# A graph network layer pair: the first phase's order written by hand, with counting spread between product matmuls

## The chip, the cores and the metric

The kernel runs on one NeuronCore of one Trainium2 chip. The metric is the device time of one execution in microseconds (us). Several executions are timed and their median is given; one further execution is recorded by the hardware profiler, and all lines of a profile come from that one.

## The reference, cut to what matters

There are 1250 nodes with 1024 features and 41,250 edges, sorted by destination. The first layer is a relational graph convolution, the second an attention layer over the same edges.

```python
h = relu(layernorm(x))                       # 1250 x 1024
nx = ln_weight * h * rsqrt(mean(h*h) + 1e-6)
out = nx @ W_root + bias                     # 1024 -> 286
for r in range(2):                           # mean over the edges of each relation
    msg = nx[src] @ W_rel[r] * (edge_type == r)[:, None]
    out += segment_sum(msg, dst) / maximum(count_r, 1)
x = x + h + elu(out) @ wo                    # 286 -> 1024
h = relu(layernorm(x))
g = h @ W                                    # 1024 -> 1024
e = exp(-leaky_relu(al[src] + ar[dst]))      # al, ar: g times two vectors
x = x + elu(segment_sum(e * g[dst], src) / (segment_sum(e, src) + 1e-5))
```

## The kernel before, in words

The 1250 nodes lie in ten tiles of up to 128 rows (T = 10, KD = 8 blocks of 128 features). A preparation sorts the edges into 110 groups of three chunks of 125 edges (NG = 110, J = 3) and makes, for each edge, a key and a low number. Then comes `fast_arm`, whose first phase (lines 469 to 572) does two independent things.

*Counting.* For each group, `count(q)` builds the number of edges between nodes as products of one-hot matrices. For each of its three chunks VectorE writes a one-hot `key` (line 496, 125 x 320, in five rotating buffers), and every two groups a one-hot `lo` (line 479). TensorE multiplies the two into `acc` (line 497), and one more matmul of 20 columns, the carry (line 500), adds what belongs to the last node of the group before. ScalarE loads the group's first node into a register (line 501) and evicts the sum of the group to that place of `cnt` (line 503). The carry's one-hots, `hot_ck`, are made in two pieces (line 486), for groups 0 to 9 and for the rest.

*Products.* For each tile, `norms` takes the statistics of x on VectorE (line 441), a square root on ScalarE, a reciprocal and `nmr` on VectorE (446, 448), then h = relu(layernorm(x)) on ScalarE (450) and the sum of its squares (510, 512). `turn` transposes h in eight matmuls (460) and copies the result to hT, one half on each of ScalarE and VectorE (463, 465). `products` multiplies hT with the joined weights wcat in sixteen steps (r = 0 and 1, k = 0 to 7, line 521; each is two matmul instructions of 429 columns in the profile). From the result, VectorE makes y0, the root part with bias (526), and the relation part is split into three bf16 parts: the first on ScalarE (531), the rest on VectorE (533), the second on ScalarE (535), the third on VectorE (536). GpSimd writes a column of ones (537). `residual` adds h to x on VectorE (554), as the sum of both is needed later. The norm's weight is multiplied into wcat ahead of all products, eight times on ScalarE (561).

The order of the instructions on each engine is that of the scheduler, which starts from the order of the calls (`some(1)` to `some(4)` groups between the stages of a tile) and moves instructions by its own estimate of when they are ready. In the order that it makes, many products stand one after the other (nine in a row at the end of most tiles), and counting stands in bunches between others. PSUM has two banks for each of two products ("mm"), three banks shared by transpositions and sums of counting ("tp"), and one that every fourth group uses ("own").

After the phase, the weights of the second layer are loaded over wcat on SP's queue (580), wo on ScalarE's (591, 598), and `means` (line 629, 600 matmuls) multiplies the counts with the bf16 parts of y. VectorE prepares wo (600 to 605) and the columns of scores (617), and the way back to 1024 columns (669) is added to x (671). The second layer's product, weights and sums follow; the change doesn't touch them.

Of the kernel before, what the change touches and what calls it, by code (L numbers as in the profile page):

```python
# [410 lines left out]
def fast_arm(tc, ctx, w_root, conv_bias, wo, w_gat, a_gat, out,  # L411
# [25 lines left out]
    def norm_relu(work, xt, n):  # L437

        st = sm.tile([128, 2, 6], F32, name="st")
        for i in range(2):  # L440
            nc.vector.bn_stats(st[:n, i, :], xt[:n, i * 512:(i + 1) * 512])  # L441
# [8 lines left out]
        nc.scalar.activation(h[:n], xt[:n], AF.Relu, bias=nmr[:n], scale=rstd[:n])  # L450
        return h

    def transposed(work, h, n, turn):

        hT = work.tile([128, KD, 128], F32, name="hT", bufs=2)
        for g in range(KD // 4):
            pt = bank("tp")
            for i in range(4):
                k = 4 * g + i
                nc.tensor.transpose(pt[:, i, :n], h[:n, k * 128:(k + 1) * 128], ident[:n, :n])  # L460
            o = hT[:, 4 * g:4 * g + 4, :n]
            if (g + turn) % 2 == 0:
                nc.scalar.activation(o, pt[:, :, :n], AF.Copy)
            else:
                nc.vector.tensor_copy(o, pt[:, :, :n])  # L465
        return hT


    y0s, ybs = {}, {}
    with ExitStack() as c1:  # L470
        hot = c1.enter_context(tc.tile_pool(name="hot", bufs=5))
        work = c1.enter_context(tc.tile_pool(name="work1", bufs=2))
        los = {}

        def count(q):

            if q % 2 == 0:
                los[q // 2] = hot.tile([PE_, 128, 2 * J], BF16, name="lo", bufs=2)
                nc.vector.tensor_tensor(  # L479
                    los[q // 2], iota_lo,  # L480
                    lows[:, q:q + 2, :].rearrange("p q j -> p (q j)")[:, None, :].to_broadcast([PE_, 128, 2 * J]),
                    ALU.is_equal,
                )
            if q in (0, 10):
                q1 = 10 if q == 0 else NG
                nc.vector.tensor_tensor(hot_ck[:, q:q1], iota_ck[:, None, :].to_broadcast([PE_, q1 - q, 2 * T]),
                                        ck[:, q:q1, None].to_broadcast([PE_, q1 - q, 2 * T]), ALU.is_equal)
            acc = (own_bank if q % 4 == 3 else bank)("acc").rearrange("p a b -> p (a b)")
            a3 = acc[:, :2 * T * W].rearrange("p (c w) -> p c w", w=W)
            if q:  # L490

                last = los[(q - 1) // 2][:, :, ((q - 1) % 2) * J + J - 1]
                carry = (a3[:, :, 0:1], last, hot_ck[:, q - 1, :, None])
            for j in range(J):
                key = hot.tile([PE_, 2 * T * W], BF16, name="key")
                nc.vector.tensor_scalar(key, iota_key, keys[:, q, j:j + 1], None, op0=ALU.is_equal)  # L496
                nc.tensor.matmul(acc[:, :2 * T * W], los[q // 2][:, :, (q % 2) * J + j], key, start=(j == 0),  # L497
                                 stop=(j == J - 1))
                if q and j == 0:
                    nc.tensor.matmul(*carry, start=False, stop=False)  # L500
            b = nc.values_load(bases[0:1, q:q + 1], engines=[mybir.EngineType.Activation],  # L501
                               min_val=0, max_val=N - 1)
            nc.scalar.activation(cnt_w[:, :, bass.ds(b, W)], a3, AF.Copy)  # L503

        def norms(t):
            n = ROWS[t]
            h = norm_relu(work, xs[t], n)
            sq = work.tile([128, D], F32, name="sq", tag="rest", bufs=1)
            ssq = small("ssq")
            nc.scalar.activation(sq[:n], h[:n], AF.Square, accum_out=ssq[:n])  # L510
            rms = small("rms")
            nc.scalar.activation(rms[:n], ssq[:n], AF.Sqrt, bias=eps6[:n], scale=1.0 / D)
            nc.vector.reciprocal(rms[:n], rms[:n])
            return h, rms

        def products(t, hT, rms):
            n = ROWS[t]
            py = ps.tile([128, 2, 512], F32, name="mm")
            for r in range(2):
                for k in range(KD):  # L520
                    nc.tensor.matmul(py[:n, r, :F + HF], hT[:, k, :n], wcat[k][:, r, :],  # L521
                                     start=(k == 0), stop=(k == KD - 1))
# [3 lines left out]
            nc.vector.scalar_tensor_tensor(  # L526
                y0[:n].rearrange("p (a b) -> p a b", a=2), py[:n, :, F:F + HF], rms[:n],
                bias[:n].rearrange("p (a b) -> p a b", a=2), op0=ALU.mult, op1=ALU.add,
            )

            nc.scalar.activation(yb[:n, 0, :, :F], py[:n, :, :F], AF.Copy, scale=rms[:n])
            rest = work.tile([128, D], F32, name="rest", tag="rest", bufs=1)[:, :2 * F].rearrange("p (r f) -> p r f", r=2)
            nc.vector.scalar_tensor_tensor(rest[:n], py[:n, :, :F], rms[:n], yb[:n, 0, :, :F],
                                           op0=ALU.mult, op1=ALU.subtract)
            nc.scalar.activation(yb[:n, 1, :, :F], rest[:n], AF.Copy)
            nc.vector.tensor_tensor(yb[:n, 2, :, :F], rest[:n], yb[:n, 1, :, :F], ALU.subtract)
            nc.gpsimd.memset(yb[:n, 0, :, F:F + 1], 1.0)

        groups = iter(range(NG))

        def some(n):
            for _ in range(n):
                q = next(groups, None)
                if q is not None:
                    count(q)

        hs_, hTs, rmss = {}, {}, {}

        def turn(t):
            hTs[t] = transposed(work, hs_[t], ROWS[t], t + 1)  # L550

        def residual(t):
            n = ROWS[t]
            nc.vector.tensor_add(xs[t][:n], xs[t][:n], hs_.pop(t)[:n])

        hs_[0], rmss[0] = norms(0)
        some(1)
        turn(0)
        hs_[1], rmss[1] = norms(1)
        for k in range(KD):  # L560
            nc.scalar.activation(wcat[k], wcat[k], AF.Copy, scale=lnw[:, k:k + 1])
            some(1)
        for t in range(T):
            residual(t)
            if t + 2 < T:
                hs_[t + 2], rmss[t + 2] = norms(t + 2)
            some(4)
            if t + 1 < T:
                turn(t + 1)
            some(3)  # L570
            products(t, hTs.pop(t), rmss.pop(t))
            some(4)

# [7 lines left out]
    work = ctx.enter_context(tc.tile_pool(name="work2", bufs=1))  # L581
# [21 lines left out]
    for i in (1, 3):  # L603
        p = slice(32 * i, 32 * i + 32)
# [311 lines left out]
    os_, oTs, hTs = {}, {}, {}  # L916

    def norm(t):
        hs_[t] = norm_relu(work, xs[t], ROWS[t])
# [4 lines left out]
    hs_ = {}  # L924
# [258 lines left out]
```

## Time and profile before

| what | value |
|---|---|
| median of 3 runs | 654.65 us (654.1 to 656.29) |
| the profiled execution | 655.82 us |
| its span | 654.0 us, so 1.8 us lie around it |
| granted TensorE clock, mean over the span | 0.987 |
| TensorE busy | 613.8 us, 94% |
| VectorE busy | 391.2 us, 60% |
| ScalarE busy | 191.8 us, 29% |
| GpSimd busy | 31.1 us, 5% |
| first key matmul of the first phase | at 15.27 us |
| first product matmul | at 27.41 us |
| first matmul of the means | at 208.59 us |

A row of the timeline gives start, duration, engine (PE is TensorE, PEld its weight loads, DVE is VectorE, ACT is ScalarE), the line of the kernel, the operation, output and inputs, shapes, and in brackets how long the engine had been idle and what ended that. Rows merge neighbouring instructions of one kind (x2, x8). Matmuls are pipelined and their ends are modelled, so what one costs is read from the distance between starts, not from its duration.

### The profile page before, as it was taken

How to read it: one execution, taken by the hardware profiler on the slowest of the kernel's cores; microseconds unless marked ns; L12 is line 12 of the kernel's file. 1: busy time of each engine (PE TensorE's matmuls, PEld its weight loads, DVE VectorE, ACT ScalarE, POOL GpSimd, SP SyncE). 2: the span in 40 equal slices, each digit the busy share in tenths (PEclk: the TensorE clock that was granted, in tenths of full speed). 3: DMA queues.
4: the chain of work that ended last, by engine and by line, in shares of the span. 5: the costliest groups of instructions: out<-in, count | busy, mean ns of one | idle time of the engine just before them, and what ended most of it. 6: DMA issues, size and time to landing. Idle time of an engine off the chain costs nothing.

```text
span 654.0 us, 7831 instructions
## 1 busy us (share of the span) xinstructions
PE 613.8 (94%) x2816; PEld 418.1 (64%) x2816; DVE 391.2 (60%) x947; ACT 191.8 (29%) x332; POOL 31.1 (5%) x42
## 2 busy tenths in 40 slices
PE   2589999999999989999799999999999999999995
PEld 1356665566665756676656788888866666666653
DVE  5599987777663399655873412214146666665632
ACT  3565555444432112420021122313112222222120
POOL 3000000000000000000000000000001111111110
PEclk9799999999999999999989999999999999999998
DMA  7900000000004610000730000000000000000011
GB/s 230 321 19 1 2 2 1 2 0 2 2 0 164 221 33 1 1 2 1 133 69 1 1 0 1 1 1 1 0 1 33 33 32 33 32 32 34 18 48 30
DMA packets 25209, 25.06 MB, mean 38 GB/s; under 512 B 14035, under 2 KB 18894, under 8 KB 25160
## 3 DMA queue, kind: packets, MB, share of 16 engines
q1 hardware_dynamic: 24059, 21.39, 10.7%
q10 hardware_dynamic: 1037, 2.90, 1.6%
q8 instruction: 24, 0.39, 0.3%
q14 instruction: 25, 0.20, 0.1%
q0 software_dynamic: 64, 0.17, 0.1%
HBM read 16.06 MB, written 5.12 MB: 32 GB/s over the span
## 4 chain that ended last, share of the span: by engine, by line
PE 80%; DVE 9%; DMA 6%; ACTq 2%; issue 1%; SPq 1%; ACT 1%; DVEq 0%
PE mm L898 16%; PE mm L521 14%; PE mm L774 11%; PE p L898 8%; PE mm L629 7%; PE acc L497 6%; PE mm L669 5%; PE z L774 4%; PE mm L703 3%; PE p L910 3%; DMA w<-in_L_gnn_W_rel_dram 2%; DVE scr L617 2%; ACTq L501 2%; DVE key L496 1%; PE p L703 1%; DMA rest_w<-in_L_gnn_wo_weight_dram 1%
## 5 line engine op out<-in xcount | busy, mean ns | idle before, releaser
L521 PE MATMUL mm<-w,hT 128*128 128x429 f32 (+1 forms) x320 | 130.3, 530 | 5.3 <-DVE hT L465 5.3
L898 PE MATMUL mm<-h,z 128*128 128x342 f32 (+1 forms) x360 | 118.5, 450 | 0.0
L898 PEld LDWEIGHTS mm<-h,z 128*128 128x128 f32 (+1 forms) x360 | 68.4, 190 | 34.9
L521 PEld LDWEIGHTS mm<-w,hT 128*128 128x128 f32 (+1 forms) x320 | 56.4, 190 | 37.8 <-issue 29.6
L496 DVE TENSOR_SCALAR key<-meta 125x320 bf16<-125x320 f16 x330 | 79.1, 296 | 2.1 <-PE acc L500 1.4
L629 PE MATMUL mm<-y,cnt 128*128 128x286 bf16 (+3 forms) x600 | 75.2, 284 | 3.2 <-DVE x L671 3.0
L497 PE MATMUL acc<-key,lo 125*128 125x320 bf16 x330 | 68.3, 314 | 5.8 <-DVE key L496 5.2
L629 PEld LDWEIGHTS <-cnt 128*128 128x128 f16 (+1 forms) x600 | 59.4, 99 | 17.7 <-issue 4.2
L503 ACT ACTIVATE cnt<-acc 128x320 f32 x110 | 49.4, 449 | 63.0 <-PE acc L497 58.2
L898 PE MATMUL p<-h,z 128*128 128x341 f32 (+1 forms) x180 | 66.1, 449 | 0.0
L497 PEld LDWEIGHTS <-lo 125*128 125x128 bf16 x330 | 35.4, 130 | 33.2 <-DVE key L496 20.9
L898 PEld LDWEIGHTS p<-h,z 128*128 128x128 f32 (+1 forms) x180 | 33.7, 188 | 17.7
L774 PE MATMUL mm<-w,a 128*128 128x257 f32 (+3 forms) x192 | 44.7, 379 | 0.0
L669 PE MATMUL mm<-wo,meta 128*128 128x512 f32 (+1 forms) x80 | 40.0, 624 | 4.5 <-DVE meta L657 4.5
L774 PEld LDWEIGHTS mm<-w,a 128*128 128x128 f32 (+1 forms) x192 | 35.9, 188 | 5.9 <-ACT h L800 0.4
L847 DVE SCALAR_TENSOR_TENSOR z<-z 128x1280 f32<-128x1280 f32 (+2 forms) x11 | 31.2, 2845 | 0.3
L450 ACT ACTIVATE h<-x,nmr,rstd 128x1024 f32<-128x1024 f32 (+1 forms) x20 | 24.7, 1237 | 20.1 <-DVE nmr L448 17.8
L441 DVE BATCH_NORM_STATS2 st<-x 128x6 f32<-128x512 f32 (+1 forms) x40 | 26.4, 673 | 7.0 <-DMA x<-in_x_dram 6.3
L479 DVE TENSOR_TENSOR lo<-meta 125x768 bf16<-125x768 f16 x55 | 30.2, 550 | 0.0
L850 ACT ACTIVATE z<-z 128x1280 f32<-128x1280 f32 (+2 forms) x11 | 12.9, 1173 | 58.8 <-DVE z L849 58.8
L888 DVE TENSOR_SCALAR inv<-mm 128x1 f32<-128x1 f32 x9 | 1.4, 158 | 47.6 <-PE mm L898 47.6
L867 POOL TENSOR_TENSOR w<-w,x 128x1024 f32<-128x1024 f32 x9 | 23.4, 2599 | 135.3 <-ACT w L863 120.7
(172 smaller groups left out, 700.9 us busy)
## 6 DMA issues: line engine op xcount, KB each, us to landing
x<-in_x_dram SPq DMA_DIRECT2D x9, 512.0 KB, 5.0
out_dram<-w SPq DMA_DIRECT2D x9, 512.0 KB, 3.0
w<-in_L_gnn_W_dram SPq DMA_DIRECT2D x8, 512.0 KB, 5.2
w<-in_L_gnn_W_rel_dram SPq DMA_DIRECT2D x8, 286.0 KB, 6.6
w<-in_L_gnn_W_root_dram SPq DMA_DIRECT2D x8, 143.0 KB, 3.8
wo<-in_L_gnn_wo_weight_dram ACTq DMA_DIRECT2D x2, 512.0 KB, 7.5
a<-in_L_gnn_a_dram ACTq DMA_DIRECT2D x2, 512.0 KB, 6.5
rest_w<-in_L_gnn_wo_weight_dram ACTq DMA_DIRECT2D x4, 120.0 KB
```

Source lines behind the costliest of these rows:

```text
L441: nc.vector.bn_stats(st[:n, i, :], xt[:n, i * 512:(i + 1) * 512])
L479: nc.vector.tensor_tensor(los[q // 2], iota_lo, lows[:, q:q + 2, :].rearrange("p q j -> p (q j)")[:, None, :].to_broadcast([PE_, 128, 2 * J]),
L496: nc.vector.tensor_scalar(key, iota_key, keys[:, q, j:j + 1], None, op0=ALU.is_equal)
L497: nc.tensor.matmul(acc[:, :2 * T * W], los[q // 2][:, :, (q % 2) * J + j], key, start=(j == 0), stop=(j == J - 1))
L503: nc.scalar.activation(cnt_w[:, :, bass.ds(b, W)], a3, AF.Copy)
L521: nc.tensor.matmul(py[:n, r, :F + HF], hT[:, k, :n], wcat[k][:, r, :], start=(k == 0), stop=(k == KD - 1))
L629: nc.tensor.matmul(pm[:n, r, :f], cnt[:k, h, r, t * 128:t * 128 + n], ybs[h][:k, s, r, :f], start=(h == 0 and s == 0), stop=(h == T - 1 an ...
L669: nc.tensor.matmul(po[:n, c, :], oT[:, i, :n], wo_of[i][:, cs], start=(i == 0), stop=False)
L703: nc.tensor.matmul(o, hT[:, k, :n], wg[k][:, c0:c1], start=(k == 0), stop=(k == KD - 1))
L774: nc.tensor.matmul(o[:a.shape[2], :c1 - c0], a[:, k, :], b[k][:, c0:c1], start=(start and k == 0), stop=(k == KH - 1), skip_group_check=no ...
L847: nc.vector.scalar_tensor_tensor(z, z, 0.1, z, op0=ALU.mult, op1=ALU.min)
L898: nc.tensor.matmul(o, z[:ROWS[t], t, :n], hs[t][:ROWS[t], c0:c1], start=(t == 0), stop=(t == T - 1))
```

## The change

Three things change, all in the first phase of `fast_arm`.

The order of TensorE, VectorE and ScalarE in this phase is the order of the calls (`manual_schedule`), with no scheduler. `count` becomes a generator that yields after each chunk (`chunks`). For every product matmul of the sixteen of a tile, the loop asks for as many chunks as keep counting in step with the products, two in nearly every case, and none for the last six products. The stages of the neighbouring tiles are placed at fixed numbers i of the sixteen: the parts of y of the tile before at 3, 5 and 8, statistics and norm of the tile two on at 6, 9, 11 and 13, transpositions and scaled copies of the next tile at 8, 9, 10 and 12. `carry_hots` is made in four pieces instead of two.

The norm's weight is no longer multiplied into wcat; it is the scale of the copies of the turned h (`scaled`), which are one copy for each block of 128 features, four on ScalarE and four on VectorE for each tile.

x + h is done by a DMA that GpSimd issues and that accumulates into x (`residual`), instead of an addition on VectorE. Apart from this, the first part of y on ScalarE stands ahead of y0 on VectorE now. SP and GpSimd keep the scheduler's order; in it, GpSimd's ten memsets stand ahead of the ten DMAs.

The diff, with the lines taken out of `count`, `norms` and `products` left out where they return unchanged:

```diff
+        c1.enter_context(tc.manual_schedule(
+            engines={mybir.EngineType.PE, mybir.EngineType.DVE, mybir.EngineType.Activation}))
...
-            if q in (0, 10):
-                q1 = 10 if q == 0 else NG
...
+        def chunks():
+
+            for q in range(NG):
+                if q % 2 == 0 and q // 2 not in los:
+                    low_hots(q)
+                if q in (10, 40, 75):
+                    carry_hots(q, {10: 40, 40: 75, 75: NG}[q])
...
+                for j in range(J):
+                    key = hot.tile([PE_, 2 * T * W], BF16, name="key")
+                    nc.vector.tensor_scalar(key, iota_key, keys[:, q, j:j + 1], None, op0=ALU.is_equal)
+                    nc.tensor.matmul(acc[:, :2 * T * W], los[q // 2][:, :, (q % 2) * J + j], key, start=(j == 0),
+                                     stop=(j == J - 1))
+                    if q and j == 0:
+                        nc.tensor.matmul(*carry, start=False, stop=False)
+                    if j == J - 1:
+                        b = nc.values_load(bases[0:1, q:q + 1], engines=[mybir.EngineType.Activation],
+                                           min_val=0, max_val=N - 1)
+                        nc.scalar.activation(cnt_w[:, :, bass.ds(b, W)], a3, AF.Copy)
+                    yield
...
+        def statistics(t, i):
+            n = ROWS[t]
+            if i == 0:
+                sts[t] = sm.tile([128, 2, 6], F32, name="st")
+            nc.vector.bn_stats(sts[t][:n, i, :], xs[t][:n, i * 512:(i + 1) * 512])
+            if i == 1:
+                mvs[t] = mv = sm.tile([128, 2], F32, name="mv")
+                nc.vector.bn_aggr(mv[:n], sts.pop(t)[:n])
+                rstds[t] = rstd = small("rstd")
+                nc.scalar.activation(rstd[:n], mv[:n, 1:2], AF.Sqrt, bias=eps5[:n], scale=1.0)
+
+        def norm(t):
+            n, mv, rstd = ROWS[t], mvs.pop(t), rstds.pop(t)
+            nc.vector.reciprocal(rstd[:n], rstd[:n])
+            nmr = small("nmr")
+            nc.vector.scalar_tensor_tensor(nmr[:n], mv[:n, 0:1], -1.0, rstd[:n], op0=ALU.mult, op1=ALU.mult)
+            hs_[t] = h = work.tile([128, D], F32, name="h")
+            nc.scalar.activation(h[:n], xs[t][:n], AF.Relu, bias=nmr[:n], scale=rstd[:n])
...
+        def scaled(t, g):
+
+            n, (hT, pts) = ROWS[t], hTs[t]
+            for i in range(4):
+                k = 4 * g + i
+                if g == 0:
+                    nc.scalar.activation(hT[:, k, :n], pts[g][:, i, :n], AF.Copy, scale=lnw[:, k:k + 1])
+                else:
+                    nc.vector.tensor_scalar(hT[:, k, :n], pts[g][:, i, :n], lnw[:, k:k + 1], None, op0=ALU.mult)
+
+        def residual(t):
             n = ROWS[t]
+            nc.gpsimd.dma_start(xs[t][:n], hs_.pop(t)[:n], accum_op=ALU.add)
+
+        def first_part(t):
+            n, py = ROWS[t], pys[t]
+            nc.vector.reciprocal(rmss[t][:n], rmss[t][:n])
+            rms = rmss[t]
...
+            nc.scalar.activation(yb[:n, 0, :, :F], py[:n, :, :F], AF.Copy, scale=rms[:n])
             nc.vector.scalar_tensor_tensor(
                 y0[:n].rearrange("p (a b) -> p a b", a=2), py[:n, :, F:F + HF], rms[:n],
                 bias[:n].rearrange("p (a b) -> p a b", a=2), op0=ALU.mult, op1=ALU.add,
             )
-
-            nc.scalar.activation(yb[:n, 0, :, :F], py[:n, :, :F], AF.Copy, scale=rms[:n])
+            nc.gpsimd.memset(yb[:n, 0, :, F:F + 1], 1.0)
+
+        def second_part(t):
...
             nc.vector.scalar_tensor_tensor(rest[:n], py[:n, :, :F], rms[:n], yb[:n, 0, :, :F],
                                            op0=ALU.mult, op1=ALU.subtract)
             nc.scalar.activation(yb[:n, 1, :, :F], rest[:n], AF.Copy)
+
+        def third_part(t):
+            n, rest, yb = ROWS[t], rests_.pop(t), ybs[t]
             nc.vector.tensor_tensor(yb[:n, 2, :, :F], rest[:n], yb[:n, 1, :, :F], ALU.subtract)
...
-            nc.vector.tensor_add(xs[t][:n], xs[t][:n], hs_.pop(t)[:n])
...
-        for k in range(KD):
-            nc.scalar.activation(wcat[k], wcat[k], AF.Copy, scale=lnw[:, k:k + 1])
-            some(1)
...
+        for i in range(2):
+            statistics(0, i)
+        low_hots(0)
+        carry_hots(0, 10)
+        norm(0)
+        some(4)
+        for g in range(2):
+            turn(0, g)
+        scaled(0, 0)
+        some(1)
+        scaled(0, 1)
+        some(1)
+        for i in range(2):
+            statistics(1, i)
+        done, ahead = 6, 6
+        SK = 2 * KD
         for t in range(T):
+            pys[t] = ps.tile([128, 2, 512], F32, name="mm")
+            for i in range(SK):
+                r, k = divmod(i, KD)
+                if t:
+                    if i == 3:
+                        first_part(t - 1)
+                    elif i == 5:
+                        second_part(t - 1)
+                    elif i == 8:
+                        third_part(t - 1)
+                if i == 6:
+                    residual(t)
+                if t == 0 and i == 1:
+                    norm(1)
+                if t == 0 and i in (3, 5):
+                    square(i // 4)
+                if t + 2 < T:
+                    if i in (6, 9):
+                        statistics(t + 2, (i - 6) // 3)
+                    elif i == 11:
+                        norm(t + 2)
+                    elif i == 13:
+                        square(t + 2)
+                if t + 1 < T:
+                    if i in (8, 10):
+                        turn(t + 1, i // 10)
+                    elif i == 9:
+                        scaled(t + 1, 0)
+                    elif i == 12:
+                        scaled(t + 1, 1)
+                nc.tensor.matmul(pys[t][:ROWS[t], r, :F + HF], hTs[t][0][:, k, :ROWS[t]], wcat[k][:, r, :],
+                                 start=(k == 0), stop=(k == KD - 1))
+                want = min(NG * J, ahead + -(-(NG * J - ahead) * (t * SK + i + 1) // (T * SK - 6)))
+                some(want - done)
+                done = max(done, want)
+        for part in (first_part, second_part, third_part):
+            part(T - 1)
```

More of the change, by code (lines that the diff above doesn't have):

```diff
@@ L472, in fast_arm @@
         work = c1.enter_context(tc.tile_pool(name="work1", bufs=2))
+        c1.enter_context(tc.manual_schedule(
+            engines={mybir.EngineType.PE, mybir.EngineType.DVE, mybir.EngineType.Activation}))
         los = {}
[L475 to L483, printed above, removed]
-            if q in (0, 10):
-                q1 = 10 if q == 0 else NG
[L486 to L503, printed above, removed]
@@ L505, in norms, with low_hots, carry_hots @@
-        def norms(t):
-            n = ROWS[t]
-            h = norm_relu(work, xs[t], n)
+        def low_hots(q):
+            los[q // 2] = hot.tile([PE_, 128, 2 * J], BF16, name="lo", bufs=2)
+            nc.vector.tensor_tensor(
+                los[q // 2], iota_lo,
+                lows[:, q:q + 2, :].rearrange("p q j -> p (q j)")[:, None, :].to_broadcast([PE_, 128, 2 * J]),
+                ALU.is_equal,
+            )
+        def carry_hots(q, q1):
+            nc.vector.tensor_tensor(hot_ck[:, q:q1], iota_ck[:, None, :].to_broadcast([PE_, q1 - q, 2 * T]),
+                                    ck[:, q:q1, None].to_broadcast([PE_, q1 - q, 2 * T]), ALU.is_equal)
@@ new lines, in chunks @@
+        def chunks():
[4 more added lines that the diff above has]
+                    carry_hots(q, {10: 40, 40: 75, 75: NG}[q])
+                acc = (own_bank if q % 4 == 3 else bank)("acc").rearrange("p a b -> p (a b)")
+                a3 = acc[:, :2 * T * W].rearrange("p (c w) -> p c w", w=W)
+                if q:
+                    last = los[(q - 1) // 2][:, :, ((q - 1) % 2) * J + J - 1]
+                    carry = (a3[:, :, 0:1], last, hot_ck[:, q - 1, :, None])
+                for j in range(J):
[10 more added lines that the diff above has]
+                    yield
@@ new lines, in fast_arm, with some @@
+        chunk = chunks()
+        def some(n):
+            for _ in range(n):
+                next(chunk, None)
+        hs_, hTs, rmss, sts, mvs, rstds, pys, rests_ = {}, {}, {}, {}, {}, {}, {}, {}
+        def statistics(t, i):
+            n = ROWS[t]
+            if i == 0:
[6 more added lines that the diff above has]
+                nc.scalar.activation(rstd[:n], mv[:n, 1:2], AF.Sqrt, bias=eps5[:n], scale=1.0)
@@ L508, in norms, with square @@
+        def norm(t):
[5 more added lines that the diff above has]
+            nc.scalar.activation(h[:n], xs[t][:n], AF.Relu, bias=nmr[:n], scale=rstd[:n])
+        def square(t):
+            n = ROWS[t]
             sq = work.tile([128, D], F32, name="sq", tag="rest", bufs=1)
@@ L509, in norms, with turn @@
             ssq = small("ssq")
-            nc.scalar.activation(sq[:n], h[:n], AF.Square, accum_out=ssq[:n])
-            rms = small("rms")
+            nc.scalar.activation(sq[:n], hs_[t][:n], AF.Square, accum_out=ssq[:n])
+            rmss[t] = rms = small("rms")
             nc.scalar.activation(rms[:n], ssq[:n], AF.Sqrt, bias=eps6[:n], scale=1.0 / D)
-            nc.vector.reciprocal(rms[:n], rms[:n])
-            return h, rms
-        def products(t, hT, rms):
-            n = ROWS[t]
-            py = ps.tile([128, 2, 512], F32, name="mm")
-            for r in range(2):
-                for k in range(KD):
-                    nc.tensor.matmul(py[:n, r, :F + HF], hT[:, k, :n], wcat[k][:, r, :],
-                                     start=(k == 0), stop=(k == KD - 1))
+        def turn(t, g):
+            if g == 0:
+                hTs[t] = work.tile([128, KD, 128], F32, name="hT", bufs=2), []
+            n, pt = ROWS[t], bank("tp")
+            hTs[t][1].append(pt)
+            for i in range(4):
+                k = 4 * g + i
+                nc.tensor.transpose(pt[:, i, :n], hs_[t][:n, k * 128:(k + 1) * 128], ident[:n, :n])
@@ new lines, in scaled @@
+        def scaled(t, g):
+            n, (hT, pts) = ROWS[t], hTs[t]
+            for i in range(4):
+                k = 4 * g + i
+                if g == 0:
+                    nc.scalar.activation(hT[:, k, :n], pts[g][:, i, :n], AF.Copy, scale=lnw[:, k:k + 1])
+                else:
+                    nc.vector.tensor_scalar(hT[:, k, :n], pts[g][:, i, :n], lnw[:, k:k + 1], None, op0=ALU.mult)
+        def residual(t):
+            n = ROWS[t]
+            nc.gpsimd.dma_start(xs[t][:n], hs_.pop(t)[:n], accum_op=ALU.add)
@@ L529, in products @@
             )
-            nc.scalar.activation(yb[:n, 0, :, :F], py[:n, :, :F], AF.Copy, scale=rms[:n])
+            nc.gpsimd.memset(yb[:n, 0, :, F:F + 1], 1.0)
+        def second_part(t):
+            n, py, yb, rms = ROWS[t], pys.pop(t), ybs[t], rmss.pop(t)
             rest = work.tile([128, D], F32, name="rest", tag="rest", bufs=1)[:, :2 * F].rearrange("p (r f) -> p r f", r=2)
+            rests_[t] = rest
             nc.vector.scalar_tensor_tensor(rest[:n], py[:n, :, :F], rms[:n], yb[:n, 0, :, :F],
@@ L535, in products @@
             nc.scalar.activation(yb[:n, 1, :, :F], rest[:n], AF.Copy)
+        def third_part(t):
+            n, rest, yb = ROWS[t], rests_.pop(t), ybs[t]
             nc.vector.tensor_tensor(yb[:n, 2, :, :F], rest[:n], yb[:n, 1, :, :F], ALU.subtract)
[L537 to L553, printed above, removed]
-            nc.vector.tensor_add(xs[t][:n], xs[t][:n], hs_.pop(t)[:n])
-        hs_[0], rmss[0] = norms(0)
-        some(1)
-        turn(0)
-        hs_[1], rmss[1] = norms(1)
-        for k in range(KD):
-            nc.scalar.activation(wcat[k], wcat[k], AF.Copy, scale=lnw[:, k:k + 1])
-            some(1)
-        for t in range(T):
[L564 to L572, printed above, removed]
+        for i in range(2):
+            statistics(0, i)
```

## The prediction, on record before the result

> **What bounds the kernel now.** First the engine table: TensorE is busy for 94% of the span, so an edit pays only where TensorE waits, runs at a lower clock or is given less to do.
>
> ```profile
> span 654.0 us, 7831 instructions
> PE 613.8 (94%) x2816; PEld 418.1 (64%) x2816; DVE 391.2 (60%) x947; ACT 191.8 (29%) x332; POOL 31.1 (5%) x42
> ```
>
> Second, the waits of TensorE between 15 and 212 us, which is the phase that the change rewrites (columns: total, times, longest). They add up to 13.5 us, and all but a little lies before 49 us.
>
> ```profile
> PE mm L521 <- DVE hT L465: 5.3, 1, 5.3
> PE acc L497 <- DVE key L496: 5.2, 4, 3.1
> PE tp L460 <- ACT h L450: 2.5, 1, 2.5
> ```
>
> Third, the timeline of the start. VectorE stands at the statistics of x tile 2, whose load has not landed, with the copy of the turned h behind it, so the first product waits until 27.41. The two halves of an early product take 1.6 us; from 33.65 on, 0.72 us (start to next start).
>
> ```profile
> 18.77 1.97 PE L460 MATMUL tp<-ident,h 128*128 128x128 f32 x8 [2.49 <-ACT h L450]
> 24.94 0.69 DVE L441 BATCH_NORM_STATS2 st<-x 128x6 f32<-128x512 f32 x1 [5.89 <-DMA x<-in_x_dram]
> 27.41 1.80 PE L521 MATMUL mm<-w,hT 128*128 128x429 f32 x2 [5.26 <-DVE hT L465]
> 33.65 0.93 PE L521 MATMUL mm<-w,hT 128*128 128x429 f32 x2
> ```
>
> Fourth, the timeline of a settled tile. Spacing of starts gives warm prices: product 0.72, key matmul 0.145, carry matmul 0.022, transposition 0.109 us. One detail matters below: a product that follows a carry directly takes 0.81 (130.53 to 131.34), not 0.72 (128.94 to 129.66).
>
> ```profile
> 128.94 0.89 PE L521 MATMUL mm<-w,hT 128*128 128x429 f32 x2
> 129.66 0.44 PE L497 MATMUL acc<-key,lo 125*128 125x320 bf16 x2
> ...
> 130.53 0.97 PE L521 MATMUL mm<-w,hT 128*128 128x429 f32 x2
> ...
> 131.34 0.57 PE L497 MATMUL acc<-key,lo 125*128 125x320 bf16 x3
> ```
>
> Fifth, how y0 (VectorE) and the bf16 y (ScalarE) of one product stand to each other: ScalarE begins at 209.35, just as VectorE ends (208.80 + 0.52), though the product was complete for both.
>
> ```profile
> 208.80 0.52 DVE L526 SCALAR_TENSOR_TENSOR y<-mm,rms,bias 98x286 f32<-98x286 f32 x1 [8.79 <-PE mm L521]
> 209.35 0.74 ACT L531 ACTIVATE y<-mm,rms 98x572 bf16<-98x572 f32 x1 [7.96 <-DVE y L526]
> ```
>
> **What the skill says.** "TensorE: Matmul & The Clock Gate", The HAM clock gate: the clock starts at half and is released after about 3.4 us of sustained work. The trace agrees: products of 1.6 us until about 32.4, 5 us after work became continuous. "PSUM — Partial Sum Buffer", PSUM bank collisions: ScalarE and VectorE may not read one bank at once, so the two accesses must be ordered. The fence above shows that order. "DMA: Bandwidth & Descriptors", SWDGE vs HWDGE vs iDMA: an accumulating DMA must be issued by GpSimd; the anatomy section prices one at 2.0 us + bytes/436e3. "SBUF — State Buffer", two separate sides: VectorE's two-port operations can keep GpSimd from writing descriptors. No row of this trace shows an accumulating DMA.
>
> **The change, part by part.** All sums are on TensorE from its first key matmul (15.27) to the first matmul of the means (208.59): 193.3 us. Warm work is 160 x 0.72 + 330 x 0.145 + 109 x 0.022 + 80 x 0.109 = 174.2. So 19.1 us are lost: by 32.57 it had done 2 products, 16 keys, 4 carries and 8 transpositions, 4.7 us of work in 17.3, a loss of 12.6; the other 6.5 are 2.6 of visible stalls and 3.9 spread thinly.
>
> *Start (gain).* The weights' 8 scalings of 1.01 us leave ScalarE, and on VectorE the reciprocal and nmr of tile 0 now stand ahead of the keys. Statistics end at 14.2, then 0.12 + 0.47 + 0.23: reciprocal at 15.05, nmr at 15.25, h at 15.4 (was 17.48) to 16.66. First key matmul 15.65. Eight cold transpositions (1.8) from about 16.9 end at 18.7; ScalarE's four scaled copies are done by 18.8, VectorE's four by 19.65 (0.19 apart, an estimate from 512 columns in 0.68 and 128 in 0.27); the sixth key follows, and product 0 starts at about 20.2. x tile 1 landed at 16.04, so its statistics do not wait, but their 1.9 us with the next low hots hold keys until 22. From there TensorE is continuous. With 3.4 to 6.8 us to warm up (the page's window, its phase free) I take 26.5; ends 24 and 29, worth 1.3 us either way. Work done by then 4.9, so the loss is 10.85 - 4.9 = 5.95.
>
> *Two keys per product.* The instructions and prices of TensorE are the same, but the written order puts a carry directly ahead of a product 44 times, against 5 in the order of before: 44 x 0.085 = 3.7 us. Bounds: 0 if the delay was chance in those five, 4.5 with the 7 carries ahead of a transposition.
>
> *ScalarE's y ahead of y0 (new wait).* In the order of the changed program y0 waits on that very ACTIVATE, by the semaphore count; the subtraction after it carries no wait. Both stand ahead of the keys of i = 3, and all keys through i = 2 are written by then, so TensorE does product 3 and then has no key. ScalarE reaches y after the last eviction of a group that ends by i = 2. Take S = start of product 3, with the last key of a group just before it: eviction at S + 0.195 (130.00 against a key start of 129.66), y 0.34 later (124.62, 124.96), lasting 0.73; y0 0.03 later; next key 0.43 after it; its matmul 0.27 after that. Sum S + 2.0; needed at S + 0.72: a stall of 1.28. If the group ends one key earlier, 1.11; if at i = 1, 0.25. In the written order the keys done by then are 46, 80, 114, 147, 181, 215, 248, 282 and 316 for tiles 1 to 9, so each of the three cases occurs three times: 3 x (1.28 + 1.11 + 0.25) = 7.9 us. Bounds: 4 if ScalarE is earlier than I have it, 10 if its register loads (0.28 + 0.15 each) delay evictions. Queued behind y0 are 2 to 5 keys, and TensorE waits for them. After it VectorE has no lead until about i = 12: its keys (0.212 apart), one low-hot (0.47) per six, rest 0.73, third part 0.66, statistics 1.4 and four scaled copies 0.8 come to about 10.4 us in slots 3 to 12, which are worth 10.3 + 0.9 of TensorE. So no further stall, but the carry hots of chunk 40 (0.8 us) fall into tile 3 at i = 6: 0.8, those of chunk 75 about 0.2. Together 1.0.
>
> *x + h by DMA.* Ten additions of 1.22 us leave VectorE, which is idle 40% of the time: worth nothing by themselves. On GpSimd's queue stand ten memsets, then the ten DMAs, then two memsets that the next phase needs long after. Each starts when its h is written; h's buffer is wanted again by the norm two tiles on, some 16 us later. Estimate 2.0 + 524288/436e3 = 3.2 us, hidden; it stays hidden up to some 15. The first ones meet the loads of x and w, whose first users come after 27 us. Lower bound 0, upper 1 us each if descriptors and VectorE hinder one another.
>
> *Scaled turned h.* Four copies of about 0.26 instead of one of 0.60 on ScalarE, 0.27 instead of 0.68 on VectorE: hidden (ScalarE is 29% busy), except in the start, counted there.
>
> *End of the phase.* After the last tile's r = 1, k = 0 product come 7 products and 4 keys now, 7 products before: 0.6 us, by which the load of the next weights starts earlier against the end. VectorE's wait for rest_w (224.36) ends that stage, so 0.6 us are gained there. The order of the later phases on VectorE, ScalarE and SP is the same; on TensorE one transposition moves by one matmul.
>
> *Sum.* 15.65 + 174.2 + 5.95 + 3.7 + 7.9 + 1.0 + 3.0 (thin losses, 3.9 before; 1.5 to 4.5) = 211.4, against 208.6: +2.8; less 0.6: +2.2. The profiled execution took 655.82 (span 654.0 and 1.8 around it) and would become 658.0. The median of the runs shown is 1.17 lower, 654.65: forecast 656.9 us.
>
> **Rivals.** *A, the new wait is covered:* ScalarE gets to y early and keys do not run out. For it: VectorE is idle for 40%, and five key buffers hold 2.6 us of products. Against it: the order puts no key of i = 3 ahead of y0. Then 656.9 - 7.9 = 649.0, faster. It decides on one point: whether y0 begins by S, so that its 0.43 and the key's 0.27 end by S + 0.72. *B, the weight loads hide:* a carry ahead of a product costs nothing, since two keys stand ahead of it: 653.2, the same within what can be told. Against it: all five cases cost 0.08 or more. *C, the accumulating DMAs hinder:* GpSimd and VectorE share a port, or the transfer outlasts h's buffer. For it: keys and low hots are what VectorE mostly does. 0.5 us in each of ten: 662. Against it: it is issued far ahead.
>
> **How the numbers follow.** A measurement here can tell 0.3% (2.0 us) from no change. Forecast 0.44 (655 to 659.5; of it 0.34 slower by more than 0.3%, 0.10 within); A 0.25, faster; B 0.18 (0.15 within, 0.03 faster); C 0.13, slower. Faster 0.28, same 0.25, slower 0.47. The forecast's own range is 655 to 659.5; the range reaches down to A's time and up into C: 649 to 660.5, leaving about 0.12 below and 0.08 above.
>
> **What would show it.** First product near 20 us and full clock by 24 to 29. In tiles 1 to 9, after product 3, TensorE waiting on a key about 1.3 us or 0.25, with y0 on VectorE starting just as ScalarE's y ends. Products after a carry at 0.80. First matmul of the means at about 211. If those gaps are missing, A holds; if products after carries take 0.72, B; if VectorE's keys stretch while GpSimd issues, or h waits on a DMA, C.

## The result, and the profile after

The changed kernel takes 659.69 us in the median of six runs (658.43 to 661.25), the kernel before, run beside it, 654.65 (654.1 to 656.29): ratio 1.0072, 95% interval 1.0054 to 1.009, so slower by 0.7%. The forecast was 656.9 in a range of 649 to 660.5, of which 655 to 659.5 was the forecast's own part. The profiled execution took 659.33 us with a span of 657.5, and the first matmul of the means starts at 212.51, against 208.59 before and 211.4 in the prediction.

The head of the page of the changed kernel says that TensorE is busy about as long as before (615.6 us against 613.8), in a span that is 3.5 us longer. The rows of keys and of key matmuls (busy us and mean ns, then idle time just before them and its cause) name the loser: TensorE waits for keys. The last row is the new DMA: its size in KB and the us from issue to landing.

```profile
span 657.5 us, 7893 instructions
PE 615.6 (94%) x2816; PEld 416.4 (63%) x2816; DVE 390.4 (59%) x969; ACT 190.9 (29%) x354; POOL 39.9 (6%) x52
...
L505 DVE TENSOR_SCALAR key<-meta 125x320 bf16<-125x320 f16 x330 | 84.0, 300 | 17.3 <-PE acc L506 9.9
L506 PE MATMUL acc<-key,lo 125*128 125x320 bf16 x330 | 76.3, 309 | 15.0 <-DVE key L505 14.9
...
x<-h POOLq DMA_DIRECT2D x9, 512.0 KB, 4.6
```

The waits of the changed kernel between 15 and 216 us (total, times, longest) give the other half of the chain: TensorE waits for keys, and VectorE, which writes them, waits for ScalarE's y ten times. Of the 14.9 us, 4.9 belong to the start; before, 5.2 in all.

```profile
DVE y L584 <- ACT y L583: 30.7, 10, 6.8
PE acc L506 <- DVE key L505: 14.9, 15, 3.5
```

The timeline of its start shows the gain. h is made at 15.49, VectorE's scaled copies follow at 18.85 with no wait for an x tile between, the first product starts at 20.46 (before, 27.41). From 25.03 a product takes 0.72 (to 25.75), and the trace has the clock at full from 24.8.

```profile
15.49 1.24 ACT L541 ACTIVATE h<-x,nmr,rstd 128x1024 f32<-128x1024 f32 x1 [0.68 <-DVE nmr L539]
...
18.85 1.13 DVE L569 TENSOR_SCALAR hT<-tp,lnw 128x128 f32<-128x128 f32 x4 [2.32 <-PE tp L559]
...
20.46 1.65 PE L649 MATMUL mm<-w,hT 128*128 128x429 f32 x2
...
25.03 0.89 PE L649 MATMUL mm<-w,hT 128*128 128x429 f32 x2
...
25.75 0.44 PE L506 MATMUL acc<-key,lo 125*128 125x320 bf16 x2
```

Before, x + h of tile 0 stood in that queue of VectorE too, between the late statistics of x tile 2 (24.94) and the copy of the turned h that the first product waited for:

```profile
25.55 1.21 DVE L554 TENSOR_TENSOR x<-x,h 128x1024 f32<-128x1024 f32 x1
```

The timeline of slot i = 3 in tile 4 shows the loss as the prediction drew it: eviction, ScalarE's y, y0 0.03 us after its end, the keys, and TensorE on the first of them at 105.40, 2.15 after product 3 began and 1.42 after that product's 0.72 were over.

```profile
103.25 0.88 PE L649 MATMUL mm<-w,hT 128*128 128x429 f32 x2
103.51 0.44 ACT L513 ACTIVATE cnt<-acc 128x320 f32 x1 [0.80 <-PE acc L506]
103.85 0.73 ACT L583 ACTIVATE y<-mm,rms 128x572 bf16<-128x572 f32 x1
104.61 0.52 DVE L584 SCALAR_TENSOR_TENSOR y<-mm,rms,bias 128x286 f32<-128x286 f32 x1 [3.06 <-ACT y L583]
105.04 0.72 DVE L505 TENSOR_SCALAR key<-meta 125x320 bf16<-125x320 f16 x3
105.40 0.34 PE L506 MATMUL acc<-key,lo 125*128 125x320 bf16 x1 [1.26 <-DVE key L505]
```

Tile 3 shows what the prediction left out: between y0 and the first key stand the next low hots, 0.46 us more.

```profile
84.23 0.52 DVE L584 SCALAR_TENSOR_TENSOR y<-mm,rms,bias 128x286 f32<-128x286 f32 x1 [3.02 <-ACT y L583]
84.67 0.55 DVE L480 TENSOR_TENSOR lo<-meta 125x768 bf16<-125x768 f16 x1
85.13 0.94 DVE L505 TENSOR_SCALAR key<-meta 125x320 bf16<-125x320 f16 x4
85.49 0.34 PE L506 MATMUL acc<-key,lo 125*128 125x320 bf16 x1 [1.76 <-DVE key L505]
```

The account below takes each distance from one matmul's start to the next on TensorE, less the prediction's warm price, from the first key matmul to the means. Work is 174.2 us in every kernel. A stall is a distance that is over its price by more than 0.15 us; the rest, the thin losses, is negative where many distances are a little below their rounded price.

| us lost | before | after | y0 first | y0 first and carry late |
|---|---|---|---|---|
| up to 32 us | 12.4 | 5.5 | 5.9 | 4.7 |
| stalls ahead of key matmuls after that | 3.7 | 12.2 | 0.9 | 1.0 |
| first halves of products behind a carry | 0.4 | 3.4 | 3.4 | 0 |
| stalls ahead of transpositions | 0 | 1.0 | 1.1 | 1.4 |
| all the rest (thin losses) | 2.7 | 0.5 | -0.4 | 0.6 |
| first matmul of the means at | 208.59 | 212.51 | 200.75 | 197.55 |

So the change gains 7 us at the start and 2 in the thin losses, and pays 8.5 in stalls ahead of keys, 3 behind carries and 1 ahead of transpositions; its first key matmul also comes 0.45 later. Of the 2 us, 1.5 lie between one key matmul and the next (0.155 us in the median before, when keys stood in bunches, 0.140 after); why, no run here tests.

### The profile page after: what moved, and what is told of

The parts are those of the page before. It is cut to its first block, busy times and chain, and to the rows that moved or that the text cites. A ratio compares the mean times of both kernels' runs of the same rounds, so it can differ in the third digit from the quotient of the medians.

```text
span 657.5 us, 7893 instructions
## 1 busy us (share of the span) xinstructions
PE 615.6 (94%) x2816; PEld 416.4 (63%) x2816; DVE 390.4 (59%) x969; ACT 190.9 (29%) x354; POOL 39.9 (6%) x52
## 4 chain that ended last, share of the span: by engine, by line
PE 82%; DVE 11%; DMA 2%; ACT 2%; issue 1%; ACTq 0%; POOL 0%; DVEq 0%; POOLq 0%
PE mm L981 16%; PE mm L649 15%; PE mm L857 11%; PE p L981 8%; PE mm L712 7%; PE acc L506 7%; PE mm L752 4%; PE z L857 4%; PE mm L786 3%; PE p L993 3%; DVE scr L700 2%; DVE key L505 1%; PE tp L559 1%; PE p L786 1%; DMA rest_w<-in_L_gnn_wo_weight_dram 1%; ACT y L583 1%
## 5 line engine op out<-in xcount | busy, mean ns | idle before, releaser
L649 PE MATMUL mm<-w,hT 128*128 128x429 f32 (+1 forms) x320 | 145.8, 540 | 0.0
L505 DVE TENSOR_SCALAR key<-meta 125x320 bf16<-125x320 f16 x330 | 84.0, 300 | 17.3 <-PE acc L506 9.9
L506 PE MATMUL acc<-key,lo 125*128 125x320 bf16 x330 | 76.3, 309 | 15.0 <-DVE key L505 14.9
L506 PEld LDWEIGHTS <-lo 125*128 125x128 bf16 x330 | 40.9, 126 | 72.9 <-issue 40.8
L649 PEld LDWEIGHTS mm<-w,hT 128*128 128x128 f32 (+1 forms) x320 | 51.7, 192 | 4.9 <-issue 3.5
L946 ACT ACTIVATE w<-mm,inv 128x684 f32<-128x684 f32 x9 | 7.5, 830 | 74.2 <-DVE w L945 74.2
L752 PEld LDWEIGHTS mm<-wo,meta 128*128 128x128 f32 (+1 forms) x80 | 15.1, 197 | 18.8 <-issue 13.1
```

The lines of the kernel that those rows point to most:

```text
L649: nc.tensor.matmul(pys[t][:ROWS[t], r, :F + HF], hTs[t][0][:, k, :ROWS[t]], wcat[k][:, r, :], start=(k == 0), stop=(k == KD - 1))
L752: nc.tensor.matmul(po[:n, c, :], oT[:, i, :n], wo_of[i][:, cs], start=(i == 0), stop=False)
```

## The experiments

Ratios are against the kernel before, run on the same chip in the same rounds; its median there was 655.3 to 655.4.

**The wait of y0.** Three runs. The first is the swap:

```diff
-            nc.scalar.activation(yb[:n, 0, :, :F], py[:n, :, :F], AF.Copy, scale=rms[:n])
             nc.vector.scalar_tensor_tensor(
                 y0[:n].rearrange("p (a b) -> p a b", a=2), py[:n, :, F:F + HF], rms[:n],
                 bias[:n].rearrange("p (a b) -> p a b", a=2), op0=ALU.mult, op1=ALU.add,
             )
+            nc.scalar.activation(yb[:n, 0, :, :F], py[:n, :, :F], AF.Copy, scale=rms[:n])
```

> The changed kernel with one swap: y0 on VectorE stands ahead of ScalarE's y, as in the kernel before. Theory (the new wait is what the changed kernel pays): the nine stalls of TensorE on a key after product 3 (10.2 us by the spacing of starts), and those two a product later where the low hots fell behind them (1.1 us), go; the subtraction at i = 5 now waits for ScalarE's y, but has about 1.4 us in hand. 659.7 - 11.3 = 648.4 us; 650.5 if the low hots and carry hots still show. Rival 1 (VectorE has no lead anyway in slots 3 to 12, so the stall only moves from product 3 to product 5): 657 to 660. Rival 2 (the time is lost in the accumulating DMAs or elsewhere, stalls were filled by other waits): within 0.3% of 659.7.

Measured: 647.64 us (645.95 to 649.06), ratio 0.9887 (0.9867 to 0.9907). The changed kernel's ratio is 1.0072, so the swap is worth 1.9%, some 12 us, and the kernel is now faster than before. In the waits of this kernel between 15 and 216 us, TensorE's are down to the start and one place; VectorE's subtraction now waits for ScalarE's y, 6.2 us in eight times, behind keys that are already written. The wait has moved to where it has cover.

```profile
PE acc L506 <- DVE key L505: 6.5, 4, 3.5
...
DVE rest L594 <- ACT y L587: 6.2, 8, 1.0
```

The second keeps the order and moves the place:

```diff
         def first_part(t):
...
-            nc.vector.scalar_tensor_tensor(
-                y0[:n].rearrange("p (a b) -> p a b", a=2), py[:n, :, F:F + HF], rms[:n],
...
         def second_part(t):
...
+            nc.vector.scalar_tensor_tensor(
+                y0[:n].rearrange("p (a b) -> p a b", a=2), py[:n, :, F:F + HF], rms[:n],
...
             nc.vector.scalar_tensor_tensor(rest[:n], py[:n, :, :F], rms[:n], yb[:n, 0, :, :F],
```

> The changed kernel with one move: ScalarE's y stays ahead of y0 and at i = 3, but y0 on VectorE is issued at i = 5, directly ahead of the subtraction, not at i = 3. Theory (what costs is that the keys of slots 3 and 4 stand behind an instruction that waits for ScalarE's y, not which of the two comes first): the keys of i = 3 and 4 no longer wait, y is finished about 0.8 us before they are used up; the gain is nearly that of the swap (12 us): 647 to 650 us. Rival (it is the access to the same PSUM bank, or ScalarE's y being early, that counts, so only the swap helps): 656 or more.

Measured: 649.2 us (647.38 to 650.49), ratio 0.9895 (0.9878 to 0.9913); means at 202.39. The interval overlaps the swap's; the 1.6 us at the means are 0.9 more of stalls ahead of keys and 0.9 ahead of transpositions. Both engines still read the same bank here, ScalarE first, and most of the gain is there. So what costs is not which of the two comes first, but the keys that stand behind the waiting instruction.

The third gives VectorE one more buffer to run ahead:

```diff
-        hot = c1.enter_context(tc.tile_pool(name="hot", bufs=5))
+        hot = c1.enter_context(tc.tile_pool(name="hot", bufs=6))
```

> The changed kernel with six buffers for keys instead of five. Theory (VectorE writes the keys of slots 3 on only after y0, whatever buffers are free): 659.7 us, within 0.3%. Rival (TensorE runs out of keys because only five can be ahead): each stall of tiles 1 to 9 shorter by one key's 0.145 us or more, 656 to 658.

Measured: 659.67 us (658.34 to 660.27), ratio 1.0057 (1.0042 to 1.0072), and the stalls ahead of key matmuls are 12.2 us as in the changed kernel. The sixth buffer stays unused where it would count, as the next keys stand behind y0 in VectorE's order.

**The carry ahead of a product.**

```diff
+                    if q and j == J - 1:
+                        nc.tensor.matmul(*carry, start=False, stop=False)
                     nc.tensor.matmul(acc[:, :2 * T * W], los[q // 2][:, :, (q % 2) * J + j], key, start=(j == 0),
-                    if q and j == 0:
-                        nc.tensor.matmul(*carry, start=False, stop=False)
```

> The changed kernel with one edit: the carry matmul of a group stands directly ahead of the third key matmul of its group, not directly behind the first, so it never stands directly ahead of a product or a transposition (count of matmuls unchanged). Theory (a product's first half takes 0.445 instead of 0.36 us behind a carry, 42 times in the trace): 659.7 - 3.8 = 655.9 us. Rival (the 0.085 us belong to the slot, with three matmuls of counting in it, not to the neighbour): 659.7. A second rival: a carry directly behind a product costs the same 0.08 us there: 657 to 660.

Measured: 658.45 us (655.31 to 660.49), ratio 1.0043 (1.003 to 1.0057): between the theory and the rival, and by its interval hardly apart from the changed kernel. The trace separates the two questions. The product's delay is the neighbour's: after 32 us, 42 first halves behind a carry took 0.441 us on average in the changed kernel and 87 behind a key 0.364; with the carry moved, all 129 behind a key took 0.364, and a carry behind a product costs that product nothing. In the timeline of the changed kernel a product behind a carry (50.65 to 51.45, 0.80):

```profile
50.62 0.18 PE L509 MATMUL acc<-meta,lo 125*128 125x20 bf16 x1
50.65 0.97 PE L649 MATMUL mm<-w,hT 128*128 128x429 f32 x2
51.45 0.44 PE L506 MATMUL acc<-key,lo 125*128 125x320 bf16 x2
```

and in that of the kernel with the carry late, one between keys and carry (50.01 to 50.73, 0.72):

```profile
50.01 0.88 PE L649 MATMUL mm<-w,hT 128*128 128x429 f32 x2
50.73 0.18 PE L507 MATMUL acc<-meta,lo 125*128 125x20 bf16 x1
50.76 0.45 PE L508 MATMUL acc<-key,lo 125*128 125x320 bf16 x2
```

But of the 3.4 us only 1.2 arrived at the means (212.51 to 211.34). Stalls ahead of keys grew from 12.2 to 13.0: the key after product 3 comes when ScalarE's y and y0 are done, and a product that ends 0.08 earlier only waits longer (tile 1: 1.17 before, 1.28 now). Another 0.8 came back in the thin losses, between the key matmuls. It shows where nothing stalls: the three kinds of slots that hold two keys, from one product to the next, took 1.043, 1.024 and 1.078 us in the changed kernel (medians of 33 each) and 0.997, 1.039 and 1.044 with the carry late, so that three slots gain 0.065 us, where the product's delay was 0.08. The start and the transpositions gave up 0.4 and 0.3. Why, these runs don't show.

The two edits together:

> Both edits at once: y0 ahead of ScalarE's y, and the carry ahead of the third key matmul. Theory: the two costs lie on TensorE one after the other, so they add: 659.7 - 11.3 - 3.8 = 644.6 us, 10 us faster than the kernel before, whose counting and products had 6.7 us of stalls and thin losses after the start. Rival (without stalls VectorE's lead becomes short and keys set the pace of the products): 650 or more, with waits of TensorE on keys all along a tile.

Measured: 645.79 us (644.09 to 646.4), ratio 0.9853 (0.9834 to 0.9873). The means start at 197.55, 3.2 earlier than with the swap alone, and 1.1 of that lies in the start. That leaves 2.1 of the carry's 3.4 us; the thin losses took 1.0 and the transpositions 0.3. In the changed kernel, with its start left out too, 1.6 arrived. So the stalls ahead of keys ate about 0.7, and some of the gain is lost between the keys with stalls or without. This rests on single traces; the medians differ by 1.9 us, and the intervals of their ratios overlap.

**x + h.** The addition on VectorE again, at i = 6, in the changed kernel and in the one with both edits:

```diff
-            nc.gpsimd.dma_start(xs[t][:n], hs_.pop(t)[:n], accum_op=ALU.add)
+            nc.vector.tensor_add(xs[t][:n], xs[t][:n], hs_.pop(t)[:n])
```

> The changed kernel with one edit: x + h is again one addition on VectorE (1.22 us each), at the same place i = 6, in place of the DMA that accumulates. Theory (the DMAs are hidden and cost nothing; VectorE comes out of the wait for y0 without a lead): VectorE's 1.22 us at i = 6 in nine tiles find about 0.9 us of lead, and the third part and statistics follow; 0.3 to 1.0 us of new stall each: 662 to 668, 664 likeliest. Rival C of the prediction (the DMAs hinder VectorE or hold h, 0.5 us each): 654 to 656. A third case (VectorE has room): 659.7.

> The kernel with y0 first and the carry late (645.8 us), with x + h as an addition on VectorE at i = 6 again. Theory (VectorE's spare time at i = 6 is under 1.2 us, as the 0.89 us of carry hots in tile 3 already cost 0.9): 0.3 to 1 us in each tile, 651 us (648 to 655). Rival (without the wait for y0 VectorE has room for the addition): 645 to 647. Rival C of the prediction (the DMAs hinder): 641 to 644.

Measured: 666.55 us (665.95 to 667.1), ratio 1.0173 (1.0155 to 1.0191), and 651.71 us (649.86 to 653.62), ratio 0.9937 (0.9918 to 0.9955): 6.9 and 5.9 us slower than the same kernels with the DMA (by the ratios, 6.6 and 5.5). Stalls ahead of key matmuls are 19.8 instead of 12.2 us in the first, 7.4 instead of 1.0 in the second. The timeline of the first, tile 4, shows the addition, the statistics and two keys in a row on VectorE, and TensorE waiting at its end:

```profile
111.20 1.22 DVE L573 TENSOR_TENSOR x<-x,h 128x1024 f32<-128x1024 f32 x1
...
112.33 0.69 DVE L528 BATCH_NORM_STATS2 st<-x 128x6 f32<-128x512 f32 x1
112.94 0.50 DVE L505 TENSOR_SCALAR key<-meta 125x320 bf16<-125x320 f16 x2
113.27 0.51 PE L506 MATMUL acc<-key,lo 125*128 125x320 bf16 x2 [0.76 <-DVE key L505]
```

**The norm's weights.** In the kernel with both edits, multiplied into wcat again, and the turned h copied without a scale; first each scaling directly ahead of its product, then three products ahead:

```diff
-            for i in range(4):
-                k = 4 * g + i
...
+            o, pt = hT[:, 4 * g:4 * g + 4, :n], pts[g][:, :, :n]
+            if g == 0:
+                nc.scalar.activation(o, pt, AF.Copy)
+            else:
+                nc.vector.tensor_copy(o, pt)
...
+                if t == 0 and i < KD:
+                    nc.scalar.activation(wcat[i], wcat[i], AF.Copy, scale=lnw[:, i:i + 1])
```

> The kernel with y0 first and the carry late (645.8 us), with the norm's weight multiplied into wcat again: eight scalings of 1.01 us on ScalarE, each placed directly ahead of its product of tile 0, and the turned h copied in two plain copies per tile, one on ScalarE and one on VectorE. Theory (most of the gain at the start comes from the written order, in which VectorE does not stand at the statistics of x tile 2 ahead of the first copy of h; the scalings cost only what ScalarE cannot do beside the products of the slow clock): 1.0 for the first product and up to 2 more where squares and h of tile 1 queue behind scalings: 647 to 649 us. Rival (the weights on h are the gain at the start, about 7 us): 651 to 654. A third case (the copies of 128 columns cost VectorE and ScalarE more than the scalings did): 643 to 645.

In the second run these last lines become:

```diff
         scaled(0, 0)
+        for k in range(3):
+            weigh(k)
...
+                if t == 0 and i + 3 < KD:
+                    weigh(i + 3)
```

> As the kernel with the weights multiplied into wcat again, but the eight scalings stand three products ahead: the first three right after ScalarE's copy of the turned h of tile 0, the others one per product. What is open after the run with one scaling directly ahead of each product (about 12 us slower): whether the work of 8.1 us on ScalarE costs the time, or that placement, in which each product waited for a scaling that stood behind an eviction, which waited for TensorE. Theory (placement): ScalarE has the time beside the slow-clock products, product 0 starts near 20.5 and no product waits for a scaling: 646 to 649 us. Rival (the work itself: ScalarE cannot do 8.1 us of scalings, h of tile 1, two squares and the evictions by the time that they are due, and evictions hold TensorE): 652 to 657.

Measured: 658.1 us (653.59 to 662.63), ratio 1.0038 (1.0019 to 1.0056), more than the rival said; and 645.21 us (644.18 to 646.14), ratio 0.9852 (0.9829 to 0.9875), the same as with the weights on h. So the time was the placement's. The timeline of the first of the two shows the lockstep: an eviction waits for a key matmul, the scaling stands behind the eviction, the product waits for the scaling, and TensorE stays at the slow clock (1.6 us for two halves, 26.52 to 28.11; full only from 38.8).

```profile
24.60 0.43 PE L508 MATMUL acc<-key,lo 125*128 125x320 bf16 x1
...
25.13 0.44 ACT L513 ACTIVATE cnt<-acc 128x320 f32 x1 [2.78 <-PE acc L508]
...
25.46 1.00 ACT L631 ACTIVATE w<-w,lnw 128x858 f32<-128x858 f32 x1
...
26.52 1.80 PE L650 MATMUL mm<-w,hT 128*128 128x429 f32 x2 [1.49 <-ACT w L631]
...
28.11 0.74 PE L508 MATMUL acc<-key,lo 125*128 125x320 bf16 x2
```

The second is not wholly free of it. In its timeline, product 7 of tile 0 waits once for its scaling, and the trace loses 6.8 us up to 32 us, against 4.7 to 6.0 in the traces with the weights on h. The means start at 198.68, against 197.55; the medians don't show a difference.

```profile
30.45 1.00 ACT L610 ACTIVATE w<-w,lnw 128x858 f32<-128x858 f32 x1
...
31.51 0.99 PE L655 MATMUL mm<-w,hT 128*128 128x429 f32 x2 [1.56 <-ACT w L610]
```

**The carry's one-hots.** In the kernel with both edits, one stall was left ahead of a key matmul, 0.96 us in tile 3.

```diff
-                if q in (10, 40, 75):
-                    carry_hots(q, {10: 40, 40: 75, 75: NG}[q])
+                if q in (10, 35, 68):
+                    carry_hots(q, {10: 35, 35: 68, 68: NG}[q])
```

> The kernel with y0 first and the carry late (645.8 us), with one more edit: the carry's one-hots are made for groups 10, 35 and 68 on instead of 10, 40 and 75, so that the pieces fall to i = 14 of tiles 2 and 5, where VectorE has time, and not to i = 6 of tile 3. Theory: the last stall of a product on a key (0.96 us in tile 3) goes: 645.0 us, which medians here can hardly tell from 645.8; the trace can. Rival (the same amount comes back at another place, as VectorE has no room there either): 645.8 and a stall in tile 2 or 5.

Measured: 643.88 us (643.15 to 645.26), ratio 0.9829 (0.9807 to 0.985), the lowest of all, with an interval that overlaps that of 645.79. The stall is 0.16. In its profiled execution the means don't come earlier (198.45), since the start and one transposition of tile 1 were 1.5 us worse there; the saving is shown, that it reaches the end isn't.

## Why the prediction was right, and where its sum was not

The sign and the two costs were as forecast. The time lies inside the stated range near its upper end, but 0.2 us above the forecast's own part of it, and by the time alone rival C (662) is as near as the forecast (656.9). It is the traces that decide between them.

Of the 2.8 us by which the forecast was low, 1.1 arise ahead of the means (212.51 against 211.4). Another 1.5 come from carrying the sum over by one profiled execution: before, it was 1.17 above its median; after, 0.36 below. That the sum came so near is in part luck: one term was 3.4 us too small, and three others were too big by 2.2 together. By its steps:

- *Start.* First key matmul 15.65 forecast, 15.73 measured; first product 20.2 and 20.46; full clock at 26.5 and by 25.0. The loss is 5.5 against 5.95; in the other traces with the weights on h it is 4.7 to 6.0, and the clock comes to full to stay between 23.6 and 26.3. The size held, but not the first of the reasons given for it: the scalings that leave ScalarE. With them back, three products ahead, the median was the same. The written order did it, in which h is made 2 us earlier and VectorE goes from nmr to keys to the copy of h without standing at an x tile that has not landed. That x + h no longer stands there is the order's doing too: with the addition back at i = 6 the start loses 6.0, no more than others. In the kernel before, the clock had come to full at 22.3 already; at 25.7, while TensorE waited for its first product, it fell back to half, until 32.5. Whether the scalings would cost something in the order of the kernel before wasn't tried.
- *Two keys per product.* 3.7 forecast, 3.4 measured. Rival B, that a carry ahead of a product costs nothing, is refuted: 42 cases at 0.08, gone when the carry moves. That it is the product's weight load which shows there wasn't tested. Moving the carry didn't win the term back whole: with the start left out, 1.6 of the 3.4 us came back in the changed kernel and 2.1 without the stalls, in part because the distances between keys grew.
- *ScalarE's y ahead of y0.* This is the mis-sized term: 7.9 forecast, bounds 4 to 10, and 11.3 measured (the swap removed 11.3 and 12 us of time). Its three cases were 1.28, 1.11 and 0.25; they are 1.42 (tile 4), 1.18 (tiles 1 and 5: 1.17, tile 9: 1.20) and 0.47 (tiles 2, 6, 7: 0.64, 0.40, 0.38), in sum 9.2. The other 2.1 are low hots that stand behind y0 in tiles 1, 3, 6 and 8, about 0.5 each. The prediction counted them in VectorE's work up to i = 12, but not in the queue between y0 and the key that TensorE waits for. (The items of that work, as it names them, come to 9.4 us and not 10.4; the rest, such as y0's 0.43, isn't named.) Rival A, the cover, is refuted: the order puts no key of i = 3 ahead of y0, and a sixth buffer changes nothing.
- *Carry hots.* 1.0 forecast; 0.68 at i = 6 of tile 3 and 0.29 at the second place.
- *Thin losses.* 3.0 forecast; 0.5, and 1.0 of transpositions, which the waits put down to ScalarE's copies of the turned h. This took back 1.5 of the 3.4 us by which the stalls were too small. The terms of the sum so stand at 15.7 + 174.2 + 5.5 + 3.4 + 11.3 + 1.0 + 1.5 = 212.6, against 212.51 in the trace.
- *x + h by DMA.* Taken as 0, and the DMA costs nothing that shows: no norm waits for h's buffer, keys average 300 ns against 296, and taking the DMA away made both kernels slower, so rival C is refuted. But "worth nothing by themselves" holds only against VectorE's 60% of the whole span. In the written order VectorE has less than 1.2 us in hand at i = 6, as the new stalls of 0.3 to 1.1 in nearly every tile show, and the ten additions cost about 6 us. The sum was untouched because it was made on the changed order; a reader who took the edit for idle would have been wrong.
- *Scaled turned h.* Hidden, as said. Its pieces are slower than estimated (four take 1.13 us on each engine, not about 0.8), and still nothing waits except twice a transposition.
- *End.* 0.6 forecast, 0.5 in the two traces (445.4 to 444.9 from the means to the end). It can't be told: over the twelve traces of this study that stretch, whose code the experiments leave alone, took 443.5 to 447.0. A part of this is TensorE's clock, which falls to half once between 313 and 344 us in every trace: for 3.4 us in four of them (443.5 to 444.2), for 6.8 in eight (444.8 to 447.0), the two compared here among these.

## What to carry to other kernels

In an order written by hand, an instruction that waits for another engine holds everything behind it on its own engine, whatever that engine's share of busy time (here VectorE, busy for 59% of the span, and some 12 us); put what the bottleneck waits for ahead of it, or the waiting instruction two slots later. To size such a stall, add up all that stands between the wait's end and the bottleneck's next input, not just the waiting instruction. And cost an edit that frees an engine against the slack at its place in the new order, not against the engine's idle share.

## What was not expected of the hardware

A float32 product of 429 columns takes 0.441 us for its first half when the matmul ahead of it is the 20-column bf16 carry, 0.364 when it is a 320-column key; a carry behind a product adds nothing to that product. The accumulating DMA of 512 KB from SBUF to SBUF lands in 4.6 us, where the price that the Trainium skill ("DMA: Bandwidth & Descriptors", the anatomy section) gives for a DMA from GpSimd, not for an accumulating one in particular, had led to an estimate of 3.2; the issue takes GpSimd 0.9. In the traces of the changed kernel and of the one with y0 first, the 15 keys that start while GpSimd issues last 341 and 340 ns on average, 298 and 297 otherwise. Most of them are no longer than others; five in each trace take 406 to 440. With ten issues of 0.9 us, that is too small to matter here.
